# A feed-forward stage with half of its features turned by DMA transposes as two float16 numbers

## The chip, the cores and the metric

The kernel runs on one core of a Trainium2 chip. The metric is the device time of one execution in microseconds (us), the median of several runs. A NeuronCore has five engines that run their own queues of instructions in order: PE (TensorE, matrix products; the load of its stationary operand is shown apart as PEld), DVE (VectorE), ACT (ScalarE), POOL (GpSimd) and SP (SyncE, which here only issues DMA transfers). They meet through semaphores: an instruction waits until others have signalled.

## The reference

The reference is a small graph network of two layers over 4096 nodes with 256 features. Each layer is an attention over a 4096 x 4096 adjacency followed by a feed-forward. The change touches only the feed-forward of layer 0, which applies one step 30 times to every row:

```python
def step(h, _):
    h = h + 0.01 * jnp.tanh(h)
    h = h * jax.nn.sigmoid(h)
    h = _layernorm(h, ln_w, ln_b)        # (h - mean) * rsqrt(var + EPS) * w + bias
    h = jnp.einsum('bsc,dc->bsd', h, W) + b
    return (h, None)
x, _ = jax.lax.scan(step, x, None, length=N_ITERS)      # 30 steps
# the layer: x = x + that of layernorm(x)
```

All inputs and the result are float32.

## The kernel before

The kernel is written with a recording layer: each line appends an instruction to an engine's queue, tiles come from pools with a number of buffers (`bufs`), and waits for data and for free buffers are put in automatically. Before the change a scheduler of that layer may move instructions of one engine past each other where it thinks that it helps.

The feed-forward keeps all 4096 rows in SBUF, in the tile `y` (128 partitions, 32 row tiles `NT`, 256 columns; scaled by 100, so that the factor 0.01 can be folded into the activations). The rows are cut into `NG` = 8 groups of `G` = 4 row tiles, 512 rows. One group in one step is a **unit**; there are 30 x 8 = 240, numbered so that all groups do step 1, then all do step 2. The loop over `at` is a software pipeline, in which several units are at different places at once. A unit goes through:

- L772, ACT: the tanh of `y` into `th`, 1024 columns a partition; L773, POOL: `th + y`.
- L778, ACT: the silu of that into `z`.
- L101 and L103, DVE (in the helper `over_std`): `bn_stats` and `bn_aggr` of each row; L105, DVE: EPS added to the variances, 4 columns; L106, POOL: the power -0.5 of them, which gives `ln_rstd`.
- L114, PE (in the helper `transposed`): eight transposes of 128x128 blocks of `z` into the PSUM tile `tp`; L813, ACT: its copy into `zT`. The matmul contracts over features, so these must lie on the partitions.
- L787, PE: eight float32 matmuls with 256 columns, two blocks of the contraction (`KC` = 2) for each of four row tiles, into `po`. In the trace each is two matmul instructions.
- L797, DVE: `po` times `ln_rstd` plus `bias`, back into `y`, four operations of 256 columns.

The weights `wT` are prepared ahead of the loop (L731 to L754): the norm's weights and bias are folded into them, and the mean over the features is taken off, so that the norm's subtraction isn't needed. `init` (L712 to L716) norms the rows of a group as they come in from DRAM, during the first eight turns of the loop. In the last step, `last` stands for `bias`, and L807 adds the layer's input rows (DVE) before they are stored to DRAM; the attention of layer 1 begins with them.

In the attention, lines L394 (DVE, two inputs in SBUF), L337 and L368 (POOL), L328, L335 and L483 (ACT), and L569 (PE, float16 matmuls with 130 columns) serve below as measured examples of operations of like kind.

Of the kernel before, what the change touches and what calls it, by code (L numbers as in the profile page):

```python
# [11 lines left out]
F32 = mybir.dt.float32  # L12
BF16 = mybir.dt.bfloat16
F16 = mybir.dt.float16
I32 = mybir.dt.int32
AF = mybir.ActivationFunctionType
OP = mybir.AluOpType
AX = mybir.AxisListType
# [3 lines left out]
P = 128  # L22
C = 256
KC = C // P
# [3 lines left out]
G = 4  # L28
EPS = 1e-5
# [6 lines left out]
TINY = 1e-30  # L36


def bcast_rows(ap, n=P):

    return bass.AP(tensor=ap.tensor, offset=ap.offset, ap=[[0, n]] + [list(x) for x in ap.ap])
# [3 lines left out]
def gnn_ffn_kernel(ctx: ExitStack, tc: tile.TileContext, a: dict, out: bass.AP):  # L45
    nc = tc.nc
# [3 lines left out]
    NG = NT // G  # L50
    GR = G * P
# [44 lines left out]
    def over_std(pool, src):  # L96

        st = pool.tile([P, G, 6], F32, name="ln_st")
        mv = pool.tile([P, G, 2], F32, name="ln_mv")
        for r in range(G):  # L100
            nc.vector.bn_stats(st[:, r, :], src[:, r, :])  # L101
        for r in range(G):
            nc.vector.bn_aggr(mv[:, r, :], st[:, r, :])  # L103
        rstd = pool.tile([P, G], F32, name="ln_rstd")
        nc.vector.tensor_scalar(rstd, mv[:, :, 1], EPS, None, op0=OP.add)  # L105
        nc.gpsimd.tensor_tensor(rstd, rstd, mhalf, OP.pow)  # L106
        return rstd, mv

    def transposed(psum, src, name="tp"):

        ps = psum.tile([P, KC, GR], F32, name=name)
        for k in range(KC):
            for r in range(G):
                nc.tensor.transpose(ps[:, k, r * P : (r + 1) * P], src[:, r, k * P : (k + 1) * P], ident)  # L114
        return ps
# [573 lines left out]

    with ExitStack() as scope:
        one = scope.enter_context(tc.tile_pool(name="f_one", bufs=1))
        wT = one.tile([P, KC, C], F32, name="wT")
        bias = one.tile([P, C], F32, name="bias")
        last = one.tile([P, C], F32, name="last")
        y = one.tile([P, NT, C], F32, name="y")
        work = scope.enter_context(tc.tile_pool(name="f_work", bufs=3))
        small = scope.enter_context(tc.tile_pool(name="f_small", bufs=6))

        x1 = {}

        def load(g):
            if g not in ahead:
                load_ahead(x1d, g)
            x1[g] = ahead.pop(g)

        def init(g):
            t = x1.pop(g)
            rstd, mv = over_std(small, t)  # L710
            rs = small.tile([P, G], F32, name="rs")
            nc.vector.tensor_scalar(rs, rstd, 100.0, None, op0=OP.mult)  # L712
            nm = small.tile([P, G], F32, name="nm")
            nc.vector.scalar_tensor_tensor(nm, mv[:, :, 0], -1.0, rs, op0=OP.mult, op1=OP.mult)
            for r in range(G):
                nc.scalar.activation(  # L716
                    y[:, g * G + r, :], t[:, r, :], AF.Identity, scale=rs[:, r : r + 1], bias=nm[:, r : r + 1]
                )

        load(0)  # L720
        load(1)
        with tc.tile_pool(name="f_prep", bufs=1) as prep, tc.tile_pool(name="f_pps", bufs=1, space=PSUM) as pps:
            ln = prep.tile([2 * KC, P], F32, name="ln")
            nc.scalar.dma_start(ln[:KC], a["L0_ffn_ln_w"].rearrange("(k p) -> k p", p=P))
            nc.scalar.dma_start(ln[KC:], a["L0_ffn_ln_b"].rearrange("(k p) -> k p", p=P))
            wr = prep.tile([P, KC, C], F32, name="wr")
            nc.scalar.dma_start(wr, a["L0_ffn_W"].rearrange("(k p) c -> p k c", p=P))
            nc.scalar.dma_start(bias, bcast_rows(a["L0_ffn_b"]))
            init(0)
            ps = pps.tile([P, 2 * KC], F32, name="ps_ln")  # L730
            nc.tensor.transpose(ps, ln, ident[: 2 * KC, : 2 * KC])  # L731
            lnT = prep.tile([P, 2 * KC], F32, name="lnT")
            nc.vector.tensor_scalar(lnT, ps, 100.0, None, op0=OP.mult)
            lbb = prep.tile([P, KC, P], F32, name="lbb")
            nc.vector.tensor_copy(lbb, lnT[:, KC:, None].to_broadcast([P, KC, P]))
            ps = pps.tile([P, KC, C], F32, name="ps_w")
            for k in range(KC):
                for o in range(KC):
                    nc.tensor.transpose(ps[:, k, o * P : (o + 1) * P], wr[:, o, k * P : (k + 1) * P], ident)
            raw = prep.tile([P, KC, C], F32, name="raw")  # L740
            nc.vector.tensor_copy(raw, ps)
            ps = pps.tile([P, C], F32, name="ps_b")
            for k in range(KC):
                nc.tensor.matmul(ps, lbb[:, k, :], raw[:, k, :], start=(k == 0), stop=(k == KC - 1))
            nc.vector.scalar_tensor_tensor(bias, bias, 100.0, ps, op0=OP.mult, op1=OP.add)

            nc.vector.tensor_scalar(last, bias, -100.0, None, op0=OP.add)
            for k in range(KC):
                nc.vector.tensor_scalar(raw[:, k, :], raw[:, k, :], lnT[:, k : k + 1], None, op0=OP.mult)
            ps = pps.tile([P, C], F32, name="ps_m")  # L750
            for k in range(KC):
                nc.tensor.matmul(ps, mean, raw[:, k, :], start=(k == 0), stop=(k == KC - 1))
            for k in range(KC):
                nc.vector.tensor_tensor(wT[:, k, :], raw[:, k, :], ps, OP.subtract)  # L754

        ps_t = scope.enter_context(tc.tile_pool(name="f_pst", bufs=2, space=PSUM))
        ps_o = scope.enter_context(tc.tile_pool(name="f_pso", bufs=2, space=PSUM))

        th, zs, rs, zT = {}, {}, {}, {}
        units = FFN_STEPS * NG  # L760
        for at in range(units + 4):
            if at < NG:
                if at + 2 < NG:
                    load(at + 2)
                if at:
                    init(at)
            if units - NG <= at - 1 < units:
                load((at - 1) % NG)
            if at < units:
                g = at % NG  # L770
                th[at] = work.tile([P, G, C], F32, name="th")
                nc.scalar.activation(th[at], y[:, g * G : (g + 1) * G, :], AF.Tanh, scale=0.01)  # L772
                nc.gpsimd.tensor_tensor(th[at], th[at], y[:, g * G : (g + 1) * G, :], OP.add)  # L773
            if 0 <= at - 2 < units:
                pt = transposed(ps_t, zs.pop(at - 2))
            if 0 <= at - 1 < units:
                z = zs[at - 1] = work.tile([P, G, C], F32, name="z", bufs=4)
                nc.scalar.activation(z, th.pop(at - 1), AF.Silu, scale=0.01)  # L778
                rs[at - 1] = over_std(small, z)[0]
            if 0 <= at - 3 < units:  # L780
                u = at - 3
                g = u % NG
                src = zT.pop(u)
                po = ps_o.tile([P, G, C], F32, name="po")
                for r in range(G):
                    for k in range(KC):
                        nc.tensor.matmul(  # L787
                            po[:, r, :],
                            src[:, k, r * P : (r + 1) * P],
                            wT[:, k, :],  # L790
                            start=(k == 0),
                            stop=(k == KC - 1),
                        )
                rstd = rs.pop(u)
                end = u >= units - NG
                for r in range(G):
                    nc.vector.scalar_tensor_tensor(  # L797
                        y[:, g * G + r, :],
                        po[:, r, :],
                        rstd[:, r : r + 1],  # L800
                        last if end else bias,
                        op0=OP.mult,
                        op1=OP.add,
                    )
                if end:
                    t = x1.pop(g)
                    nc.vector.scalar_tensor_tensor(  # L807
                        t, y[:, g * G : (g + 1) * G, :], 0.01, t, op0=OP.mult, op1=OP.add
                    )
                    nc.sync.dma_start(rows_of(x2d, g), t)  # L810
            if 0 <= at - 2 < units:
                zT[at - 2] = work.tile([P, KC, GR], F32, name="zT")
                nc.scalar.copy(zT[at - 2], pt)  # L813


    RH = a["L1_ffn_router_w1"].shape[1]
# [456 lines left out]
```

## Time and profile before

| | |
|---|---|
| median of 3 runs | 3517.87 us (3514.87 to 3520.3) |
| profiled execution | span 3522.9 us, mean clock of TensorE 0.977 of full |
| the feed-forward's matmuls (L787) | first at 812.36, last ends at 1877.63 us |
| of one unit, mean durations | L772 1047 ns, L773 2367, L778 1060, L101 414 (x4), L103 154 (x4), L105 302 (median), L106 1019 (median), L813 1011, L797 470 (x4) |
| other rows used below | L807 1210 ns (1024 columns), L394 1233 (1040 columns), L368 240, L328 582 (512 columns from PSUM), L335 301, L483 712 (512 columns) |

Over the whole span the page gives PE 92% busy, DVE 85%, ACT 75%, POOL 32%. These are averages over stages with different limits, so the feed-forward has to be read by itself.

In a line of a timeline the columns are: start in us, how long in us, engine, line, operation, what it writes and reads with shapes, how many in a row, and in brackets how long the engine sat idle before it and who ended that wait. Operations of one engine overlap a little at their ends (about 0.08 us on DVE), so durations of instructions in a row add up to somewhat more than the time that they take. In the chain of waits, a line is a start, a length, and the engine and line that the end of the stretch hung on.

### The profile page before, as it was taken

How to read it: one execution, taken by the hardware profiler on the slowest of the kernel's cores; microseconds unless marked ns; L12 is line 12 of the kernel's file. 1: busy time of each engine (PE TensorE's matmuls, PEld its weight loads, DVE VectorE, ACT ScalarE, POOL GpSimd, SP SyncE). 2: the span in 40 equal slices, each digit the busy share in tenths (PEclk: the TensorE clock that was granted, in tenths of full speed). 3: DMA queues.
4: the chain of work that ended last, by engine and by line, in shares of the span. 5: the costliest groups of instructions: out<-in, count | busy, mean ns of one | idle time of the engine just before them, and what ended most of it. 6: DMA issues, size and time to landing. Idle time of an engine off the chain costs nothing.

```text
span 3522.9 us, 80529 instructions
## 1 busy us (share of the span) xinstructions
PE 3251.1 (92%) x33403; PEld 2927.4 (83%) x33403; DVE 3009.0 (85%) x6007; ACT 2638.3 (75%) x2934; POOL 1136.6 (32%) x899
## 2 busy tenths in 40 slices
PE   7889999996999999999999899999989999995995
PEld 4788888885888888888886799999879999984784
DVE  7999999997877777777778899999889999996445
ACT  3888888886766666666664999999799999982221
POOL 4111001005877777777772000000120000002662
PEclk9999999998999999999999999999999999997997
DMA  7997786501000000000006030321313140414224
GB/s 148 174 221 172 161 205 127 161 23 55 1 1 1 1 1 1 1 1 1 1 1 228 17 115 29 115 85 59 117 61 102 57 133 26 127 50 144 82 89 182
DMA packets 280198, 288.44 MB, mean 82 GB/s; under 512 B 97149, under 2 KB 230426, under 8 KB 279834
## 3 DMA queue, kind: packets, MB, share of 16 engines
q1 hardware_dynamic: 198770, 224.18, 19.3%
q0 software_dynamic: 73920, 52.97, 9.9%
q10 hardware_dynamic: 7144, 6.16, 0.6%
q8 instruction: 263, 4.31, 0.5%
q14 instruction: 101, 0.83, 0.1%
HBM read 248.01 MB, written 68.81 MB: 90 GB/s over the span
## 4 chain that ended last, share of the span: by engine, by line
PE 40%; DVE 33%; issue 14%; POOL 5%; ACT 5%; DMA 2%; another core or an unknown queue 0%; ACTq 0%; DVEq 0%; POOLq 0%; SPq 0%
PE po L787 22%; DVE m L617 17%; PE acc L569 9%; PE tp L114 6%; ACT st L483 3%; DVE rows L632 3%; DVE m L632 2%; POOL yd L1193 2%; POOL gx L1127 2%; DVE v L382 1%; DVE u L496 1%; DVE ms L229 1%; DVE u L506 1%; DVE u L510 1%; DVE u L518 1%
## 5 line engine op out<-in xcount | busy, mean ns | idle before, releaser
L569 PE MATMUL acc<-vals,m 128*128 128x130 f16 (+1 forms) x19456 | 1721.2, 232 | 73.0 <-DVE m L632 43.4
L483 ACT ACTIVATE st<-f1b,f2b 128x1024 bf16<-128x1024 f32 (+2 forms) x1664 | 1659.1, 1073 | 98.2 <-DVE m L617 91.7
L569 PEld LDWEIGHTS <-m 128*128 128x128 bf16 x19456 | 1516.2, 98 | 171.1 <-DVE m L632 65.9
L617 DVE TENSOR_TENSOR m<-st,m 128x2048 bf16<-128x2048 bf16 (+2 forms) x832 | 928.9, 1134 | 15.0 <-ACT st L483 14.9
L787 PE MATMUL po<-wT,zT 128*128 128x256 f32 x3840 | 874.5, 381 | 13.5 <-ACT zT L813 12.5
L787 PEld LDWEIGHTS po<-wT,zT 128*128 128x128 f32 x3840 | 713.7, 191 | 104.6 <-ACT zT L813 15.0
L773 POOL TENSOR_TENSOR th<-th,y 128x1024 f32<-128x1024 f32 x240 | 567.9, 2367 | 192.7 <-ACT th L772 192.7
L569 PE MATMUL acc<-vals,rows 128*128 128x130 f16 x5120 | 614.3, 221 | 15.3 <-DVE rows L632 15.3
L106 POOL TENSOR_TENSOR ln_rstd<-ln_rstd,mhalf 128x4 f32<-128x4 f32 x272 | 286.8, 1055 | 872.1 <-DVE ln_rstd L105 652.6
L569 PEld LDWEIGHTS <-rows 128*128 128x128 bf16 x5120 | 490.1, 96 | 20.8 <-DVE rows L632 20.4
L101 DVE BATCH_NORM_STATS2 ln_st<-z 128x6 f32<-128x256 f32 x960 | 337.9, 414 | 190.6 <-ACT z L778 190.6
L813 ACT COPY zT<-tp 128x1024 f32<-128x1024 f32 x240 | 242.8, 1011 | 323.1 <-PE tp L114 323.1
L632 DVE TENSOR_TENSOR rows<-m,m 128x2048 bf16<-128x2048 bf16 x320 | 391.7, 1224 | 10.2
L797 DVE SCALAR_TENSOR_TENSOR y<-po,ln_rstd,bias 128x256 f32<-128x256 f32 x928 | 378.7, 470 | 5.7 <-PE po L787 4.9
L778 ACT ACTIVATE z<-th 128x1024 f32<-128x1024 f32 x240 | 254.3, 1060 | 18.1 <-POOL th L773 17.8
L114 PE MATMUL tp<-ident,z 128*128 128x128 f32 x1920 | 250.1, 273 | 9.0 <-ACT z L778 8.1
L772 ACT ACTIVATE th<-y 128x1024 f32<-128x1024 f32 x240 | 251.2, 1047 | 4.8 <-DVE y L797 4.8
L114 PEld LDWEIGHTS tp<-ident,z 128*128 128x128 f32 x1920 | 224.9, 141 | 35.9 <-ACT z L778 10.7
L209 POOL DMA_DIRECT2D rows<-in_adj_dram x80 | 72.9, 912 | 490.9 <-PE tp_m L219 478.3
L632 DVE TENSOR_TENSOR m<-m,m 128x1792 bf16<-128x1792 bf16 (+1 forms) x200 | 202.2, 1011 | 13.0 <-PE acc L569 0.5
L462 POOL MEMSET hs<- 128x4 f32 x3 | 0.3, 102 | 603.4 <-DVE u L513 583.1
L1155 ACT COPY w<-ew 128x512 f32 x37 | 22.7, 618 | 129.1 <-PE ph L1162 66.5
(217 smaller groups left out, 2420.1 us busy)
## 6 DMA issues: line engine op xcount, KB each, us to landing
m<-edges SPq DMA_DIRECT2D x32, 2048.0 KB
rows<-in_adj_dram POOLq DMA_DIRECT2D x64, 448.0 KB
edges<-ms SPq DMA_DIRECT2D x64, 448.0 KB
m<-edges SPq DMA_DIRECT2D x16, 1792.0 KB
f1b<-fd SPq DMA_DIRECT2D x32, 512.0 KB
rows<-x1d SPq DMA_DIRECT2D x16, 512.0 KB
y<-yd SPq DMA_DIRECT2D x16, 512.0 KB
f1b<-fd SPq DMA_DIRECT2D x16, 448.0 KB
```

Of the source, the lines that this page charges most:

```text
L101: nc.vector.bn_stats(st[:, r, :], src[:, r, :])
L106: nc.gpsimd.tensor_tensor(rstd, rstd, mhalf, OP.pow)
L114: nc.tensor.transpose(ps[:, k, r * P : (r + 1) * P], src[:, r, k * P : (k + 1) * P], ident)
L483: nc.scalar.activation(steps[at][:, s, :w], f1b[c, h][:, :w], AF.Relu, bias=f2b[:, 2 * q + s, h : h + 1], scale=BIG)
L569: nc.tensor.matmul(acc[:, i, cols], lhs[:, s, rows], v[:, cols], start=(j == 0 and n_ == 0), stop=(j == NT - 1 and n_ == 1), skip_group_ch ...
L617: nc.vector.tensor_tensor(m1[:, :, :w], st[:, :, :w], m, OP.logical_and if turned(q) else OP.min)
L632: nc.vector.tensor_tensor(m2[:, :, :w], m, m1[:, :, :w], OP.subtract)
L772: nc.scalar.activation(th[at], y[:, g * G : (g + 1) * G, :], AF.Tanh, scale=0.01)
L773: nc.gpsimd.tensor_tensor(th[at], th[at], y[:, g * G : (g + 1) * G, :], OP.add)
L778: nc.scalar.activation(z, th.pop(at - 1), AF.Silu, scale=0.01)
L787: nc.tensor.matmul(po[:, r, :], src[:, k, r * P : (r + 1) * P], wT[:, k, :], start=(k == 0), stop=(k == KC - 1),)
L797: nc.vector.scalar_tensor_tensor(y[:, g * G + r, :], po[:, r, :], rstd[:, r : r + 1], last if end else bias, op0=OP.mult, op1=OP.add,)
```

## The change

The contraction of 256 features is cut in two halves. The first 128 features are turned by PE as before: four transposes for a unit, one float32 matmul for each row tile. The second 128 features leave PE's transposes. Each value of `z` there is scaled by a power of two and written as the sum of two float16 numbers: ACT makes the upper one (rounded), DVE the remainder, the lower one, in one operation that reads `z` and the upper half. One DMA transpose, issued by SP, turns both, 128 x 1024 float16 numbers, from SBUF to SBUF. The weights of this half are also split in two float16 numbers, and four float16 matmuls (upper and lower of `z` with upper and lower of the weights) take the place of one float32 matmul. The purpose is to take transposes off PE.

The rest goes with it:

- The scales are found from the weights and the bias ahead of the loop, so that float16 can't overflow; `under`, their inverse, is multiplied into the row factors by POOL.
- EPS is added by ACT, no longer by DVE.
- POOL's addition of `th` gets a wait for the lower half's operation on DVE.
- The loop's instructions on PE, DVE, ACT and POOL stand in written order; no scheduler moves them.
- The pipeline is one turn deeper: transposes at `at - 3`, matmuls at `at - 4`, `y` at `at - 5`.
- In the last step the factor 0.01 is in `last` and `under`, and POOL adds the layer's input, no longer DVE.
- Three groups of rows, not two, are asked for ahead, and their norms are measured a turn earlier.

```diff
-        wT = one.tile([P, KC, C], F32, name="wT")
+        wT = one.tile([P, C], F32, name="wT")
+        w16 = one.tile([P, 2, C], F16, name="w16")
...
-            nc.vector.tensor_scalar(last, bias, -100.0, None, op0=OP.add)
+            nc.vector.tensor_scalar(last, bias, -100.0, 0.01, op0=OP.add, op1=OP.mult)
...
+            nc.vector.tensor_tensor(sq, raw, raw, OP.mult)
...
+                nc.tensor.matmul(ps, mean, sq[:, k, :], start=(k == 0), stop=(k == KC - 1))
...
+            nc.vector.tensor_reduce(far[:, 0:1], ps, axis=AX.X, op=OP.max)
...
+            nc.gpsimd.tensor_tensor(far[:, 1:2], far[:, 0:1], mhalf[:, :1], OP.pow)
...
+            nc.vector.tensor_scalar(wT, raw[:, 0, :], scale[:, :1], scale[:, 1:], op0=OP.mult, op1=OP.mult)
+            nc.vector.tensor_scalar(w16[:, 0, :], raw[:, 1, :], scale[:, 1:], None, op0=OP.mult)
+            nc.vector.scalar_tensor_tensor(
+                w16[:, 1, :], raw[:, 1, :], scale[:, 1:], w16[:, 0, :], op0=OP.mult, op1=OP.subtract
+            )
...
-        for at in range(units + 4):
+        with tc.manual_schedule(engines={PE, DVE, Activation, Pool}):
+            for at in range(units + 6):
...
+                u = at - 3
+                    for r in range(G):
+                        nc.tensor.transpose(pt[:, r * P : (r + 1) * P], z[:, r, :P], ident)
+                u = at - 5
+                    for r in range(G):
+                        nc.vector.scalar_tensor_tensor(y[...], po[:, r, :], rstd[:, r : r + 1], last if end else bias, ...)
+                u = at - 2
+                    nc.scalar.activation(z, th.pop(u), AF.Silu, scale=0.01)
+                    z16 = work.tile([P, 2, G, P], F16, name="z16", bufs=4)
+                    nc.scalar.activation(z16[:, 0], z[:, :, P:], AF.Identity, scale=scale[:, :1])
+                    lower = nc.vector.scalar_tensor_tensor(
+                        z16[:, 1], z[:, :, P:], scale[:, :1], z16[:, 0], op0=OP.mult, op1=OP.subtract
+                    )
+                    zT16[u] = work.tile([P, 2 * G, P], F16, name="zT16", bufs=4)
+                    nc.sync.dma_start_transpose(zT16[u], z16.rearrange("p s r c -> p (s r c)"))
+                if at < units:
+                    nc.scalar.activation(th[at], y[:, g * G : (g + 1) * G, :], AF.Tanh, scale=0.01)
+                    ins = nc.gpsimd.tensor_tensor(th[at], th[at], y[:, g * G : (g + 1) * G, :], OP.add)
+                    if lower is not None:
+                        tc.add_manual_dep(ins.ins, lower.ins.name, ..., reason="the port that both use")
...
+                u = at - 3
+                    nc.scalar.copy(zT[u], pt)
+                    nc.scalar.activation(rs[u], mvs.pop(u)[:, :, 1], AF.Identity, bias=eps)
+                    nc.gpsimd.tensor_tensor(rs[u], rs[u], mhalf, OP.pow)
+                    nc.gpsimd.tensor_tensor(rs[u], rs[u], under[:, int(u >= units - NG), :], OP.mult)
...
+                u = at - 4
+                    for r in range(G):
+                        nc.tensor.matmul(po[:, r, :], src[:, r * P : (r + 1) * P], wT, start=True, stop=False)
+                        for part in range(2):
+                            for other in range(2):
+                                nc.tensor.matmul(po[:, r, :], src16[:, part * G + r, :], w16[:, other, :], ...)
...
-                    nc.vector.scalar_tensor_tensor(
-                        t, y[:, g * G : (g + 1) * G, :], 0.01, t, op0=OP.mult, op1=OP.add
-                    )
+                    nc.gpsimd.tensor_tensor(t, t, y[:, g * G : (g + 1) * G, :], OP.add)
```

## The prediction

> **What bounds the kernel now.** I went from the page to the stage. The page's table by 40 slices shows one stage, from about 800 to 1880 us, with PE at 9 tenths in nearly every slice and no DMA traffic; it is the feed-forward. So I read the table by stretches in the middle of it (PE, PEld, DVE, ACT, POOL busy, granted clock, DMA share, GB/s), then the chain of waits of the same stretch in order of time.
>
> ```profile
> 1200.00:1400.00 200.00, 200.00 (x1110) 178.64 (x1109) 159.46 (x601) 134.94 (x140) 156.61 (x93) 1.00 0.00 1
> ```
> ```profile
> 1203.16 0.87 PE tp L114 x8
> 1204.04 3.46 PE po L787 x16
> 1207.49 0.87 PE tp L114 x8
> 1208.36 3.46 PE po L787 x16
> ```
>
> PE is busy for all of the 200 us at full clock, and the chain holds nothing but PE: a unit (512 rows, one step) is 8 transposes in 0.87 us and 16 matmul instructions in 3.46 us, together a **period of 4.33 us**, 240 times 1039 us. Per instruction that is 109 ns a transpose and 216 ns a float32 matmul instruction of 256 columns (two for each matmul of the source). The others per period, from the first line times 4.33/200: DVE 3.45, POOL 3.39, ACT 2.92 us. PE is the bound, but DVE and POOL are only a fifth below it, and the change loads both.
>
> The timeline of one period, and one from the attention after this stage, show a second coupling:
>
> ```profile
> 1302.37 2.37 POOL L773 TENSOR_TENSOR th<-th,y 128x1024 f32<-128x1024 f32 x1 [0.84 <-ACT th L772]
> ...
> 1304.46 0.30 DVE L105 TENSOR_SCALAR ln_rstd<-ln_mv 128x4 f32<-128x4 f32 x1
> ...
> 1304.84 1.02 POOL L106 TENSOR_TENSOR ln_rstd<-ln_rstd,mhalf 128x4 f32<-128x4 f32 x1
> ```
> ```profile
> 1902.46 1.23 DVE L394 SCALAR_TENSOR_TENSOR vals<-vals,v 128x1040 f16<-128x1040 f16 x1
> 1902.72 1.84 POOL L106 TENSOR_TENSOR ln_rstd<-ln_rstd,mhalf 128x4 f32<-128x4 f32 x1 [3.23 <-DVE ln_rstd L105]
> ...
> 1903.69 1.23 DVE L394 SCALAR_TENSOR_TENSOR vals<-vals,v 128x1040 f16<-128x1040 f16 x1
> ```
>
> In the first, the tiny EPS addition on DVE ends at 1304.76, just as POOL's long addition ends at 1304.74; it takes 0.30 us where it elsewhere takes 0.15. In the second, the power on POOL takes 1.84 instead of 1.02 us: it waits until DVE's two-input operation ends at 1903.69. But the next two-input operation then runs its usual 1.23 us beside the rest of that power. So the power holds what they share only for a moment, not for its whole 1.02 us.
>
> **What the Trainium skill says.** "SBUF — State Buffer", section "Who interferes with whom", says that a DVE instruction with two SBUF inputs and a GpSimd instruction that reads SBUF exclude each other, and the second waits. The trace agrees with the wait (0.82 us above), but the power lets go early. "DMA: Bandwidth & Descriptors", section "Latency and other measured facts", gives 261 GB/s for DMA transposes in one kernel; "VectorE: DVE Perf Modes", section "The three transpose paths", gives 1309 ns for one 128x128 transpose by DMA. No run here has a DMA transpose. "TensorE: Matmul & The Clock Gate", section "Wait — 56ns, not 53.3ns?", gives N columns / 2.4 GHz + 2.5 ns for a bf16 matmul. The 216 ns of a float32 instruction of 256 columns fits two such passes.
>
> **The change, part by part, for one unit.**
>
> PE loses 4 of 8 transposes: 0.435 us remains. Half of the contraction stays float32: 8 instructions, 3.46/2 = 1.73 us. The other half becomes 16 float16 matmuls of 256 columns. Low bound by the TensorE page: 109 ns. High bound by the nearest row, the attention's float16 matmul of 130 columns: 109 of them in 7.81 us at 784.82 us, 72 ns each, scaled by columns 141 ns. I take 109, since 72 ns for 130 columns must hold a fixed part (the weight load), which 256 columns hide: 16 x 0.109 = 1.75 us. **PE: 0.435 + 1.73 + 1.75 = 3.91 us** (4.43 at the high bound).
>
> DVE loses the EPS addition (0.30, of which 0.21 alone) and gains the lower half's two-input operation, 512 columns: from the rows of 256 columns (470 ns) and 1024 columns (1210 ns, L807) 0.96 ns a column, 0.72 us, or 0.64 back to back. 3.45 - 0.21 + 0.64 = **3.88 us**, within 1% of PE.
>
> ACT gains the upper half (512 columns with a pointer scale: 0.58 to 0.71 us by the copies of 512 columns and the 712 ns of L483) and the EPS addition (0.30 by L335), and its copy of the turned half shrinks from 1.01 to 0.58: 2.92 - 0.43 + 0.6 to 0.7 + 0.2 to 0.3 is about 3.4 us. Hidden under PE.
>
> POOL keeps 2.37 + 1.02 and gains a multiply of 4 columns, 0.24 us by L368: 3.63 us plus gaps, about **3.75 us**. Its long addition now waits for the lower half. Behind it on POOL queue the power and the multiply, for which the y of two steps later waits. Once DVE has done the lower half, it needs bn_stats, bn_aggr and y (1.32 + 0.28 + 1.54 = 3.14 us) before it wants the next one, and the addition is over after 2.37 + 0.1. So they interleave; only the multiply may be held up some 0.2 us, and POOL still closes its round in under 3.9.
>
> The DMA transpose (256 KB in, 256 KB out) is new, on an idle queue. Its latency L, from the lower half's end to data in place, is the great unknown. The queue before holds nothing it would wait for. In written order a ring closes over three steps: lower half of unit u, transpose, matmuls of u, y of u, lower half of u+3 behind it on DVE. Hence 3T >= L + 3.46 + 1.63 + 0.72 + about 0.4 of hand-overs, **T >= (L + 6.2)/3**. With T = 3.91 it stays hidden up to L = 5.5 us; T is back at 4.33 with L = 6.8. Low bound: 1.0 us of data at 261 GB/s plus 1.3, L = 2.3. High bound: eight 128x128 blocks one after another, 8 x 1.309 = 10.5 us. I take about 4 us, since blocks spread over 16 DMA engines should overlap; both ends stay in the range.
>
> Written order itself costs nothing in the steady state as long as each engine has slack in its step. I take T = 3.95 rather than 3.91 for hand-overs between four engines that all stand at 3.4 to 3.9: 240 x (4.33 - 3.95) = **91 us gained**.
>
> Outside the steady state: before, the first matmul stands at 812.36 and the last ends at 1877.63, 1065 us for 1039 us of periods, so 26 us go in the start, waiting for loads and the initial norms. The preparation gets a serial chain: square, a matmul at low clock (1.2), a maximum, a power (1.0), some dozen tiny DVE operations (0.15 each plus hand-overs), the splitting of the weights: about 8 us ahead of the first upper half. One step more of pipeline and L delay the first matmul by about 4 us more. Part lies beside the loads; I book 8 us. The last sums go from DVE (1.21 us each) to POOL (2.37 by L773); only the last is exposed, and the next stage waits for its store: 2 us. Sum: 3517.9 - 91 + 8 + 2 = **3437 us**.
>
> **Rivals.**
>
> Small gain. Four engines near the same load with in-order waits do not mesh, T = 4.2: -31 + 10, about 3497. For it: DVE at 3.88 has no slack, and each wait for another engine breaks its back-to-back overlap of 0.08 us. Against it: before, 190 us of DVE idle time had one cause, ACT's z, and it recovered every period.
>
> The transpose bounds, slower. L = 8 gives T = 4.73: +97 + 10, about 3625; L = 10.5, or a queue that takes one transpose only after another, T = 5.6 and some 3830. For it: nothing in the trace shows the rate, and the 261 GB/s are of another kernel. Against it: the DMA engines are idle in this stage.
>
> PE or the shared port bounds, slower. Float16 at 141 ns gives T = 4.43; power and multiply keeping DVE's lower half out for their whole length gives 2.37 + 1.02 + 0.24 + 0.72 + 0.1 = 4.45. Either: +29 + 10, about 3556. Against: the 1.23 us at 1903.69, and the fixed part in 72 ns.
>
> **How the numbers follow.** Forecast 0.61, small gain 0.13, transpose 0.18, PE or port 0.08. Faster by over 0.2% (under 3511) takes the first and most of the second: 0.72. Within 0.2%: 0.03, where small gain and a transpose near L = 6.8 meet. Slower: 0.25. The forecast's spread is 3400 (T = 3.91 and a start no longer than before) to 3465 (T = 4.05). Upward the range must take in the third rival, to 3570; beyond lies most of the transpose case, 0.17.
>
> **What would show it.** Right: in mid-stage PE still 100% busy, pieces of 4 transposes in 0.44 us and 20 matmuls' worth in 3.47 us, DVE above 95%, POOL's addition released by the lower half, and no matmul released by a DMA. Wrong: idle time ahead of the matmuls with the turned float16 tile as releaser (transpose); float16 matmuls of over 120 ns (PE); the lower half on DVE longer than 0.8 us or the power longer than 1.1 us in every period (port); a first matmul later than 830 us (preparation).

## The result and the profile after

The changed kernel takes **3432.9 us** (median of 4 runs, 3431.05 to 3437.91), the kernel before 3519.1 us in the same comparison. The ratio is **0.9759, 95% interval 0.9742 to 0.9776**: 86 us faster.

The table by stretches, middle of the stage (PE, PEld, DVE, ACT, POOL busy, granted clock, DMA share, GB/s), of the changed kernel:

```profile
1200.00:1400.00 200.00, 200.00 (x1430) 163.75 (x1429) 199.68 (x665) 173.44 (x256) 191.42 (x154) 1.00 0.38 68
```

PE is still never idle, and now DVE is busy for 99.8% and POOL for 95.7% of the time. The chain of waits of the changed kernel, one unit from it:

```profile
1201.61 0.44 PE tp L831 x4
1202.05 0.43 PE po L896 x2
1202.48 0.44 PE po L899 x4
1202.92 0.43 PE po L896 x2
1203.35 0.44 PE po L899 x4
...
1205.53 0.44 PE tp L831 x4
```

Four transposes, then four times two float32 instructions and four float16 ones: 1201.61 to 1205.53 is a period of **3.92 us** where it was 4.33. Sixteen float16 matmuls take 4 x 0.44 us, 109 ns each; the loads of their stationary operands (98 ns each in the trace) run beside them and add nothing. The timeline of the same kernel shows how the other engines fit in:

```profile
1301.30 0.74 DVE L853 SCALAR_TENSOR_TENSOR z<-z,scale,z 128x512 f16<-128x512 f32 x1
1301.69 0.41 POOL L886 TENSOR_TENSOR z_rs<-z_rs,under 128x4 f32<-128x4 f32 x1
...
1302.18 2.37 POOL L862 TENSOR_TENSOR th<-th,y 128x1024 f32<-128x1024 f32 x1
...
1304.50 1.01 POOL L885 TENSOR_TENSOR z_rs<-z_rs,mhalf 128x4 f32<-128x4 f32 x1
...
1305.22 0.74 DVE L853 SCALAR_TENSOR_TENSOR z<-z,scale,z 128x512 f16<-128x512 f32 x1
```

The lower half (L853) runs undisturbed, 0.74 us. The multiply (L886) comes while it runs and takes 0.41 us instead of the 0.20 that it takes in e7 and e12. It ends at 1302.10, and the long addition follows at 1302.18, with the way free: the next lower half starts 0.67 us after the addition's end, while the power runs, and is not held up by it. Below, "what the two share" stands for whatever it is that makes a two-input operation of DVE and an operation of POOL wait for each other.

No matmul waits for a DMA from 1200 to 1400 us. In a table by quarters of a microsecond the transposes show only as bursts of about 1.4 us on the DMA engines; the burst of the lower half that ended at 1302.04 is over at about 1304.7.

### The profile page after: what moved, and what is told of

It reads as the page before. It is cut to its first block, busy times and chain, and to the rows that moved or that the text cites. A ratio compares the mean times of both kernels' runs of the same rounds, so it can differ in the third digit from the quotient of the medians.

```text
span 3430.3 us, 84143 instructions
## 1 busy us (share of the span) xinstructions
PE 3156.7 (92%) x34367; PEld 2771.3 (81%) x34367; DVE 3115.3 (91%) x6016; ACT 2754.3 (80%) x3414; POOL 1242.3 (36%) x1149
## 4 chain that ended last, share of the span: by engine, by line
PE 36%; DVE 35%; issue 13%; POOL 7%; ACT 6%; DMA 2%; DVEq 0%; POOLq 0%; ACTq 0%; SPq 0%
DVE m L617 17%; PE acc L569 10%; PE po L899 9%; PE po L896 9%; ACT st L483 4%; DVE rows L632 3%; PE tp L831 2%; DVE m L632 2%; POOL th L862 2%; PE ph L1262 1%; POOL yd L1293 1%; DVE z_st L874 1%; DVE y L838 1%; POOL gx L1227 1%; DVE u L496 1%
## 5 line engine op out<-in xcount | busy, mean ns | idle before, releaser
L899 PE MATMUL po<-w,zT 128*128 128x256 f16 x3840 | 580.4, 274 | 5.7 <-DMA zT<-z 5.7
L896 PE MATMUL po<-wT,zT 128*128 128x256 f32 x1920 | 579.1, 384 | 6.4 <-ACT zT L881 6.4
L899 PEld LDWEIGHTS <-zT 128*128 128x128 f16 x3840 | 377.6, 98 | 169.7 <-DMA zT<-z 7.3
L838 DVE SCALAR_TENSOR_TENSOR y<-po,z_rs,bias 128x256 f32<-128x256 f32 x928 | 384.8, 477 | 4.2 <-PE po L899 2.1
L874 DVE BATCH_NORM_STATS2 z_st<-z 128x6 f32<-128x256 f32 x960 | 335.5, 412 | 0.0
L896 PEld LDWEIGHTS po<-wT,zT 128*128 128x128 f32 x1920 | 292.5, 193 | 16.4 <-ACT zT L881 7.8
L106 POOL TENSOR_TENSOR ln_rstd<-ln_rstd,mhalf 128x4 f32<-128x4 f32 x32 | 42.1, 1317 | 656.8 <-DVE ln_rstd L105 641.9
L850 ACT ACTIVATE z<-th 128x1024 f32<-128x1024 f32 x240 | 251.2, 1046 | 7.3 <-POOL th L862 6.6
L885 POOL TENSOR_TENSOR z_rs<-z_rs,mhalf 128x4 f32<-128x4 f32 x240 | 244.5, 1019 | 0.0
L881 ACT COPY zT<-tp 128x512 f32<-128x512 f32 x240 | 140.8, 587 | 116.2 <-PE tp L831 116.2
```

What stands on the lines that cost most here:

```text
L838: nc.vector.scalar_tensor_tensor(y[:, g * G + r, :], po[:, r, :], rstd[:, r : r + 1], last if end else bias, op0=OP.mult, op1=OP.add,)
L850: nc.scalar.activation(z, th.pop(u), AF.Silu, scale=0.01)
L874: nc.vector.bn_stats(st[:, r, :], z[:, r, :])
L885: nc.gpsimd.tensor_tensor(rs[u], rs[u], mhalf, OP.pow)
L896: nc.tensor.matmul(po[:, r, :], src[:, r * P : (r + 1) * P], wT, start=True, stop=False)
L899: nc.tensor.matmul(po[:, r, :], src16[:, part * G + r, :], w16[:, other, :], start=False, stop=(part == 1 and other == 1),)
```

## The experiments

The ratios below are to the kernel before, in the same comparison, since from one comparison to the next its median moved by up to 15 us (3508 to 3523). A time "against the changed kernel" is the difference of the two ratios times 3520 us; with the intervals as they are, a difference of less than some 7 us can't be told from none.

### Where the gain comes from: PE, and the order

**e1_all_on_pe.** All transposes and float32 products back on PE, the rest of the change kept (without a lower half, POOL's addition has nothing to wait for on DVE).

```diff
-                    for r in range(G):
-                        nc.tensor.transpose(pt[:, r * P : (r + 1) * P], z[:, r, :P], ident)
+                    pt = transposed(ps_t, z)            # eight transposes
...
-                    (z16, lower, dma_start_transpose; four float16 matmuls per row tile)
+                    (two float32 matmuls per row tile, L787's form)
```

> All 256 features turned by PE again, all products float32; no float16 halves, no DMA transposes. Kept: written order, EPS on ACT, the multiply and the last sums on POOL, the longer preparation. Theory (the gain is PE's lighter load): the period goes back to 4.33 us, 240 x (4.33 - 3.92) = 98 us above the changed kernel, about 3531 us, so some 12 us slower than before, since the longer start and end stay. Rival (written order or the EPS move brought the gain): stays below 3480 us.

Measured: 3524.3 us (3521.2 to 3530.7), ratio 1.0006 (0.9997 to 1.0015): no difference from before. The middle of the stage:

```profile
1200.00:1400.00 200.00, 200.00 (x1113) 178.72 (x1112) 150.34 (x555) 142.63 (x185) 165.67 (x139) 1.00 0.00 1
```

PE is never idle and does 1110 to 1113 matmul instructions in 200 us, as before the change. So written order, EPS on ACT and the sums on POOL bring nothing by themselves; the steady gain is the four transposes that PE no longer does. The 12 us that I expected for a longer start and end are not there: 2 us, interval -1 to 5.

**e2_scheduler.** The changed kernel without the written order.

```diff
-        with tc.manual_schedule(engines={PE, DVE, Activation, Pool}):
+        if True:
```

> The changed kernel without the written order: the scheduler may move instructions of PE, DVE, ACT and POOL. Theory (with PE at 100, DVE at 99.8 and POOL at 96 per cent there is no slack for an order that puts another operation ahead): 20 to 80 us slower than the changed kernel, 3453 to 3513 us. Rival (order hardly matters, the loads decide): within 6 us of 3433.

Measured: 3657.8 us (3655.9 to 3660.3), ratio 1.0385 (1.0368 to 1.0402): 4% slower than the kernel before, and 220 us slower than the changed kernel, nearly three times what I allowed at most. Its timeline shows why:

```profile
1299.44 2.35 POOL L855 TENSOR_TENSOR th<-th,y 128x1024 f32<-128x1024 f32 x1
1299.57 2.77 DVE L846 SCALAR_TENSOR_TENSOR z<-z,scale,z 128x512 f16<-128x512 f32 x1
...
1304.57 0.67 PE L889 MATMUL po<-wT,zT 128*128 128x256 f32 x2 [1.61 <-DVE z_mv L869]
```

The scheduler moves every second lower half so far back that another unit's addition on POOL starts just before it: it then takes 2.77 us, all behind it on DVE is late, and PE waits. From 1200 to 1400 us the 41 lower halves take 1.78 us on average where they took 0.74, 1.04 us more; the period over the 200 middle units is 4.85 us where it was 3.92, 0.93 more. So this wait accounts for the loss, and the chain of waits of this stretch holds hardly any PE. With the order that this scheduler chose the transposes lose; they gain with an order that keeps these two operations apart.

**e3_eps_on_dve.** EPS back on DVE, behind `bn_aggr`.

```diff
-                    nc.scalar.activation(rs[u], mvs.pop(u)[:, :, 1], AF.Identity, bias=eps)
+                    nc.vector.tensor_scalar(rs[u], mvs.pop(u)[:, :, 1], EPS, None, op0=OP.add)
```

> EPS added by DVE again, in the written place behind bn_aggr, nothing else changed. Theory (the small fp32 operation is shut out by POOL's long addition, which runs from the end of the lower half for 2.37 us): a period is the sum of lower half 0.66, hand-over 0.14, addition 2.37, EPS 0.15, y 1.54, hence 4.86 us, +225 us, about 3658 us, and L884's operation takes about 1 us on DVE. Rival (only DVE's load counts): 0.15 us more a period, +36 us, about 3470 us.

Measured: 3633.0 us, ratio 1.0314 (1.0293 to 1.0334), +195 us. Groups by line (busy, mean ns) in the stretch from 1200 to 1400 us:

```profile
L884 DVE TENSOR_SCALAR z_rs<-z_mv 128x4 f32<-128x4 f32 x43 | 43.9, 1021 | 0.0
```

Four columns take 1.02 us on average instead of 0.15; each ends when POOL's addition ends. The period is 4.75 us, by the sum on record 4.86. In the kernel before, the same operation cost 0.30 us and nothing on the bound, since there it met only the last 0.28 us of the addition. What makes this tiny operation dear is the moment at which it comes, and the new order moves that moment. The move to ACT is therefore no detail of the change: without it, in this order, the change loses.

**e4_no_port_wait.** The explicit wait taken out.

```diff
-                    if lower is not None:
-                        tc.add_manual_dep(ins.ins, lower.ins.name, ...)
```

> The wait of POOL's addition for the lower half is taken out (the two share no data). Theory (the two exclude each other and POOL's addition is ready 2.4 us earlier, at the end of the tanh): the addition starts first, the lower half is held up by it, and the period becomes 4.2 to 4.35 us, +65 to +105 us, 3500 to 3540 us, with the lower half at 1.2 us or more instead of 0.74. Rival (POOL and DVE fall into step by themselves): within 10 us of 3433.

Measured: 3439.6 and 3461.0 us, ratio 0.9795 (0.9759 to 0.9831). The steady period stays at 3.92 us, with 200.00 of 200 us on PE. The profile is of the run of 3439.6 us, and its stage is over as early as that of the changed kernel; why the other run took 21 us more is open, and with two runs so far apart a small cost of leaving the wait out can't be excluded. My theory of a longer period was wrong, and the timeline shows what I left out:

```profile
1302.47 0.74 DVE L853 SCALAR_TENSOR_TENSOR z<-z,scale,z 128x512 f16<-128x512 f32 x1
1302.72 0.55 POOL L879 TENSOR_TENSOR z_rs<-z_rs,under 128x4 f32<-128x4 f32 x1
...
1303.23 2.37 POOL L862 TENSOR_TENSOR th<-th,y 128x1024 f32<-128x1024 f32 x1
```

The multiply stands ahead of the addition in POOL's queue and is itself held until the lower half ends (0.55 us). So in this order the addition doesn't come too early: the small operation does the work of the wait. The explicit wait is a safeguard, not the source of the gain.

### What bounds now

**e5_less_pe** leaves out the product of the two lower halves, **e6_less_dve** half of the statistics, **e7_less_both** both.

```diff
-                        for part in range(2):
-                            for other in range(2):
+                        for part, other in ((0, 0), (0, 1), (1, 0)):        # e5, e7
...
-                    for r in range(G):
+                    for r in range(0, G, 2):                                # e6, e7
                         nc.vector.bn_stats(st[:, r, :], z[:, r, :])
```

> Left out: the product of the two lower halves, so three float16 matmuls instead of four for each row tile; PE has 0.44 us less a period, 3.48 us. Theory (DVE at 99.8 per cent is a second bound right below PE): the period falls only to DVE's 3.90 us, at most 6 us less than the changed kernel, 3427 to 3433 us. Rival (PE alone bounds, DVE's business is partly waiting): down to POOL's 3.76 us or lower, 38 us or more less, below 3395 us.

> Left out: the statistics of every second row tile (its neighbour's are used), so DVE has two bn_stats less a period, 0.7 us. Theory (PE bounds): the period stays at 3.92 us, within 5 us of the changed kernel, 3428 to 3438 us, with DVE at about 82 per cent. Rival (DVE bounds and PE's queue only looks full): faster by 20 us or more.

> Both of these left out. Theory (two bounds next to each other, POOL is the third): the period falls to POOL's round, 2.37 + 1.02 + 0.20 and its gaps, 3.65 to 3.8 us, 30 to 65 us less than the changed kernel, 3370 to 3403 us. Rival (each of the two alone bounds nothing, the ring over the DMA transpose does): stays within 10 us of 3433.

e5: 3413.5 us (3410.1 to 3415.6), ratio 0.9701 (0.9685 to 0.9717), 20 us less than the changed kernel, between the two expectations (at most 6, and 38 or more). The middle of the stage:

```profile
1200.00:1400.00 200.00, 194.94 (x1264) 149.12 (x1262) 200.00 (x687) 178.72 (x264) 191.10 (x158) 1.00 0.41 71
```

The period is 3.80 us, and the chain of waits is DVE almost throughout. So DVE is the next bound, 3% below PE, where I had put it at 0.5%. Where the 0.12 us were hidden, two timelines show, first of the changed kernel, then of e5:

```profile
1303.27 0.36 DVE L876 BATCH_NORM_AGGREGATE z_mv<-z_st 128x2 f32<-128x6 f32 x4
1303.64 1.66 DVE L838 SCALAR_TENSOR_TENSOR y<-po,z_rs,bias 128x256 f32<-128x256 f32 x4
```
```profile
1302.90 0.37 DVE L876 BATCH_NORM_AGGREGATE z_mv<-z_st 128x2 f32<-128x6 f32 x4
1303.18 1.63 DVE L838 SCALAR_TENSOR_TENSOR y<-po,z_rs,bias 128x256 f32<-128x256 f32 x4
```

In e5 `y` starts 0.09 us before the last `bn_aggr` ends: operations of one engine overlap at their ends. In the changed kernel `y` starts only after that end, so this overlap is lost: `y` starts 0.37 us behind the first `bn_aggr` instead of 0.28, which is 0.09 of the 0.12 us. DVE is waiting there, though the table counts it as busy. (With less for DVE to do, in e6 below, this wait comes into the open: DVE waits 32 us of the 200 at `y` for PE's products.)

e6: 3430.6 us (3425.5 to 3431.4), ratio 0.9747 (0.9731 to 0.9763), within the noise of the changed kernel, as the theory said, with DVE busy for 83% and the period at 3.92 us. PE bounds the changed kernel.

e7: 3459.8 us (3453.6 to 3461.3), ratio 0.9836 (0.9820 to 0.9852): **slower** than each of the two, with less work than either. Neither theory had that. Its timeline:

```profile
1302.57 2.37 POOL L862 TENSOR_TENSOR th<-th,y 128x1024 f32<-128x1024 f32 x1
...
1304.23 1.26 DVE L853 SCALAR_TENSOR_TENSOR z<-z,scale,z 128x512 f16<-128x512 f32 x1
...
1304.90 1.47 POOL L885 TENSOR_TENSOR z_rs<-z_rs,mhalf 128x4 f32<-128x4 f32 x1
...
1306.44 0.20 POOL L886 TENSOR_TENSOR z_rs<-z_rs,under 128x4 f32<-128x4 f32 x1
...
1306.59 2.36 POOL L862 TENSOR_TENSOR th<-th,y 128x1024 f32<-128x1024 f32 x1
```

DVE, with less to do and not held back by PE, is at its lower half before the addition ends (1304.94). It waits (1.26 us), gets what the two share ahead of the power, and now the power waits (1.47 instead of 1.02 us). Addition, lower half, rest of the power, multiply follow each other: 4.02 us.

**e12_stats_first** tests that reading: e7's work, but on DVE the statistics ahead of the lower half.

```diff
                     nc.scalar.activation(z16[:, 0], ...)
+                    (bn_stats, bn_aggr)
                     lower = nc.vector.scalar_tensor_tensor(z16[:, 1], ...)
...
-                    (bn_stats, bn_aggr)
```

> As e7_less_both (the product of the lower halves and half of the statistics left out), but DVE takes the statistics ahead of the lower half. In e7 DVE is so early that its lower half waits for the end of POOL's addition (1.26 instead of 0.74 us) and then goes ahead of the power, which waits in its turn (1.46 instead of 1.02): addition, lower half, rest of the power and multiply one after another, 4.02 us. Theory (it is this order at what both share): with 0.7 + 0.3 us of statistics first, the lower half comes just behind the start of the power, which holds up nothing any more, and the period falls to POOL's own round, 3.65 to 3.75 us, 65 to 90 us less than e7: a ratio of 0.958 to 0.966 to the kernel before, 3370 to 3400 us where before takes 3519. Rival (something else holds e7 at 4.02): within 12 us of e7, a ratio of 0.980 to 0.987.

Measured: 3360.6 us (3358.8 to 3362.0), ratio **0.9539 (0.9523 to 0.9555)**, 105 us less than e7 by the ratios, with the same instructions. That is even below the range on record (0.958 to 0.966). Its timeline:

```profile
1301.26 2.37 POOL L869 TENSOR_TENSOR th<-th,y 128x1024 f32<-128x1024 f32 x1
...
1303.59 1.01 POOL L884 TENSOR_TENSOR z_rs<-z_rs,mhalf 128x4 f32<-128x4 f32 x1
1303.86 0.72 DVE L860 SCALAR_TENSOR_TENSOR z<-z,scale,z 128x512 f16<-128x512 f32 x1
1304.68 0.20 POOL L885 TENSOR_TENSOR z_rs<-z_rs,under 128x4 f32<-128x4 f32 x1
1304.84 2.36 POOL L869 TENSOR_TENSOR th<-th,y 128x1024 f32<-128x1024 f32 x1
```

The lower half starts 0.27 us after the power and lies wholly beside it; neither is longer than alone. POOL works almost without a gap, 3.58 us a period, and is the bound. The 0.45 us that the power waited in e7 (1.47 against 1.02) are the whole difference of the two periods, 4.02 and 3.58. It is the order at what the two share, and not the amount of work, that made e7 slow. (e6, e7 and e12 leave out needed statistics and are no versions to use.)

### The slack of the DMA transpose

**e8_late_lower.** The lower half one turn later.

```diff
                 u = at - 2      # silu, upper half
...
+                u = at - 3
                     lower = nc.vector.scalar_tensor_tensor(zl16[:, 1], zl[:, :, P:], ...)
                     nc.sync.dma_start_transpose(zT16[u], ...)
```

> The lower half of a unit is made one turn later (same work), so that the DMA transpose has one turn instead of two before the matmuls. With the DMA traffic of the changed kernel (bursts of about 1.4 us that end some 2.8 us after the lower half's end) I put L at 2.8 us. Theory (the ring of waits, now over two turns: L, matmuls behind the first float16 one 3.03, y 1.66, lower half 0.66, hand-overs 0.3): period (2.8 + 5.65) / 2 = 4.2 us, +70 us, 3480 to 3520 us, with PE's float16 matmuls waiting for the DMA in each period. Rival (L is so short that one turn is enough): within 8 us of 3433. If L were the 4 us of the prediction: period 4.8 us, 3640 us.

Measured: 3579.2 us, ratio 1.0174 (1.0153 to 1.0194), slower than expected (3480 to 3520 us). From 1200 to 1400 us matmuls wait 24 us for the transpose, and the loads of their stationary operands 36 us. The period is 4.55 us on average (44 units in 200 us). From the timeline L can be read where a matmul waits:

```profile
1299.37 10.04 SPq L861 DMA_TRANSPOSE zT<-z  x3
...
1302.46 0.61 PE L904 MATMUL po<-w,zT 128*128 128x256 f16 x4 [0.77 <-DMA zT<-z]
```

The first transpose is released at 1299.37, just as the lower half ends, and its matmul starts at 1302.46: **L = 3.1 us**. The ring gives (3.1 + 5.65) / 2 = 4.4 us, and the turns come in pairs of 3.9 and 4.9 us whose mean is just that. What makes 4.55 of it is that L isn't always 3.1, as three pieces of the chain of waits show:

```profile
1202.38 4.45 DMA zT<-z
1212.58 3.04 DMA zT<-z
1221.38 3.75 DMA zT<-z
```

Of the 24 waits of a float16 matmul for a transpose in this stretch, 15 end 3.1 to 3.2 us after the lower half's end and 9 end 3.5 to 4.9 us after it, and the turns with these take 5.2 to 5.6 us. Among the DMA packets of this trace from 930 to 1700 us, all 20 bursts of the transpose that last over 1.8 us overlap packets of the queues that load instructions, and 22 of the 150 shorter ones do. That points to a cause; no run here tests it.

With two turns, as the change has it, the slack is 3.9 us more, and even the longest L seen, 4.9 us, is under the 5.5 us of the prediction's ring. That is why nothing waits there.

### Start and end

**e9_sums_split** puts the last sums of the first three groups on DVE, **e10_factors_early** writes the row factors of `init` at the head of a turn, **e11_best** has both, and e5's omission.

```diff
-                    nc.gpsimd.tensor_tensor(t, t, y[...], OP.add)
+                    (nc.vector if at < units else nc.gpsimd).tensor_tensor(t, t, y[...], OP.add)   # e9, e11
...
             for at in range(units + 6):
+                if at + 1 < NG:
+                    factors(at + 1)                # rs and nm, taken out of init; e10, e11
```

> The last sums of the first three groups go to DVE, the other five stay on POOL. In the changed kernel these three turns take 6.3 us instead of 3.92, since POOL then has two long additions (2 x 2.37 + 1.02 + 0.20). Theory (POOL bounds these turns): with the sums on DVE they take DVE's 3.9 + 1.2 us and some waiting behind POOL's addition, 3 to 5 us less, 3428 to 3430 us. Rival (the sum on DVE is shut out by POOL's addition and holds up all behind it): no gain, 3432 to 3437 us.

> In the first turns the row factors of the incoming group (L726 and L728, tiny DVE operations) are written at the head of the turn, ahead of the lower half, so ahead of POOL's addition. In the changed kernel they are shut out by that addition (2.31 and 2.24 us in the preparation, 0.7 to 1.1 us in the turns) and ACT waits 16 us in all for them before it can bring rows in. Theory (this chain sets the 7.4 us turns of the start): 6 to 14 us less, 3419 to 3427 us. Rival (the start waits for the rows' loads or ACT's own work): within 4 us of 3433.

> Both of these, and the product of the two lower halves left out as in e5_less_pe (three float16 matmuls for each row tile). Theory (steady state, start and end are separate stretches and their savings add): 19 + 6 to 14 + 3 to 5 us less than the changed kernel, 3395 to 3405 us. Rival (what is won at the start or end was waiting for the same thing): 3405 to 3414 us.

e9: 3423.2 us (3420.7 to 3425.4), ratio 0.9758 (0.9745 to 0.9772): no gain that stands out of the noise, and the wait that the rival expected is there. The sum has two inputs in SBUF and meets POOL's addition, in its timeline:

```profile
1760.76 2.36 POOL L862 TENSOR_TENSOR th<-th,y 128x1024 f32<-128x1024 f32 x1
...
1762.13 2.08 DVE L912 TENSOR_TENSOR rows<-rows,y 128x1024 f32<-128x1024 f32 x1
1763.08 1.99 POOL L885 TENSOR_TENSOR z_rs<-z_rs,mhalf 128x4 f32<-128x4 f32 x1
```

2.08 instead of 1.2 us, the power behind it 1.99: turns of 5.8 us instead of 6.3. By the last products of the attention's preparation (L308, at 1850.29 against 1852.09) 2 us of that are left.

e10: 3414.1 us (3411.0 to 3415.4) in the same comparison as e9, which equals the changed kernel: 9 us less, ratio 0.9731 (0.9718 to 0.9745). In the changed kernel the start has lines like these (timeline; the first two are in the preparation, the others in a turn of the loop):

```profile
803.31 2.31 DVE L726 TENSOR_SCALAR rs<-ln_rstd 128x4 f32<-128x4 f32 x1 [0.33 <-POOL ln_rstd L106]
...
809.21 2.24 DVE L728 SCALAR_TENSOR_TENSOR nm<-ln_mv,rs 128x4 f32<-128x4 f32 x1
...
829.00 1.10 DVE L726 TENSOR_SCALAR rs<-ln_rstd 128x4 f32<-128x4 f32 x1
...
830.33 2.07 ACT L730 ACTIVATE y<-rows,nm,rs 128x256 f32<-128x256 f32 x4 [2.01 <-DVE nm L728]
```

Operations of four columns take 1.1 to over 2.2 us, since they wait for POOL's addition, and ACT waits for them. e10 leaves the two in the preparation as they are (2.30 and 2.24 us); in the turns the factors now stand ahead of the addition and take 0.17 us each. ACT waits 8 instead of 16 us for them, and the first matmuls of the 21st unit start at 916.24 instead of 923.57.

e11: 3390.2 us (3387.3 to 3392.2), ratio **0.9667 (0.9654 to 0.9681)**: the fastest version that keeps the computation but for the product of the two lower halves, 32 us ahead of the changed kernel, which was expected to be 28 to 38. The savings add: 20 of e5, 10 of e10 and none to speak of from e9.

## Why the prediction was right

3437 was forecast, 3432.9 came. The mechanism is the one that was forecast: PE still bounds, and its period falls by the four transposes. That the sum came within 4 us is partly luck, as the points on start and end show. Point by point:

- **PE's 3.91 us a unit**: 3.92 measured. The choice of 109 ns for a float16 matmul of 256 columns, against 141, was right: 16 in 1.75 us. The formula that the Trainium skill gives for bf16 ("TensorE: Matmul & The Clock Gate", section "Wait — 56ns, not 53.3ns?") comes to 109 ns for 256 columns, and the trace agrees for float16.
- **DVE 3.88**: too high by 0.08; it is 3.80 when it bounds (e5). The lower half took 0.74 us, 0.72 was forecast. So DVE had a margin of 3% to PE, not 1%, and the hand-overs, for which I added 0.03 us a period, cost nothing: 7 us of the sum.
- **ACT 3.4 and POOL 3.75**: 200 us hold 51 units with 173.44 us of ACT's work and 191.42 us of POOL's, so 3.40 and 3.75 us, as forecast; the multiply is held up by 0.2 us, as forecast. One sign on record isn't seen: the trace shows POOL's addition behind the multiply, and not released by the lower half. The lower half holds up the multiply (e4).
- **L of about 4 us**: 3.1 us in most and up to 4.9 us in some of the turns of e8, under the 5.5 that the steady state allows. The rival with eight blocks one after another, 10.5 us, is refuted.
- **What the two share**: that a power, once begun, holds up nothing, taken from two lines of the attention, decided for the forecast, and e12 shows it in the stage itself. But a power that comes while DVE's operation runs waits for it. The rival of 4.45 us, with all of it one after another, was not wrong in kind: e7 has its chain at 4.02 us. In the changed kernel PE's period keeps the lower half late enough: it does so even where DVE has less to do (e6), and no longer where PE has less to do as well (e7).
- **Written order**: "costs nothing in the steady state" was too weak. It is what makes the change a gain (e2, against the order that the scheduler chose).
- **Start and end, 10 us**: too small by about 6. The last products of the attention's preparation (L308) start at 1852.09 instead of 1933.64: 82 us are left of the 98 that 240 periods gain.
- **Of these 16 us, the start** cost 5 at most, where 8 were booked. The first matmul stands at 828.17 instead of 812.36, but that is no loss of 16 us, since the kernel before has its waits behind its first matmul (turns of up to 9.3 us, against 7.4). At the 21st unit the changed kernel is 3 us ahead (923.57 against 926.80), where 20 periods gain 8. e1, with the same preparation and its first matmul at 827.49, is as early there (923.49) with the old period. The row factors, which I had not looked at, are held up in the kernel before too (2.30 us at 813.87), so what e10 wins on them is a chance that was left rather than a cost of the change. (Also, `y` comes two turns later than before, at `at - 5` instead of `at - 3`; "one turn deeper" holds for the transposes and the matmuls.)
- **The end** cost some 12 us, where 2 were booked. At the 221st unit the changed kernel is 85 us ahead (1707.56 against 1792.64). The 20 periods that follow should add 8; instead it loses 1 by its last matmul (1793.3 against 1877.63) and 3 more on the way to L308. Some 7 of the 12 lie in three turns of the end (6.1 to 6.3 instead of 3.92 us), where POOL has two long additions in one turn. I wrote that only the last sum is exposed. The last unit's matmuls also wait 1.8 us for their transpose.
- **What cancels**: start and end took about 6 us more than booked, the hand-overs 7 us less. That is the luck in the 4 us.
- The medians differ by 86 us, and the two profiled executions by 92.6 us (3522.9 and 3430.3), since that of the kernel before took 7 us more than its median. Of the 92.6, some 8 arise after 3200 us, in the last stage, whose gathers the change doesn't touch. I leave these few microseconds open.

## What to carry to other kernels

When several engines stand within a few per cent of the bound, ask of each pair that can shut each other out which comes first in a period: the same instructions gave 0.984 or 0.954 of the time before, 105 us apart, by their order alone (e7, e12), and taking work away made a kernel slower. Look for tiny operations on an engine whose neighbour runs long instructions: where the two exclude each other, as here, the price of the tiny one is the neighbour's remaining time, and it changes when any change moves the moment at which it comes. The DMA transpose beside the bound engine cost nothing in the steady state, since its latency fits in the turns of the pipeline; measure that latency by taking a turn away, and look at the slowest of them and not only at the usual one.

## What was unexpected of the hardware

- A DMA transpose of 128 x 1024 float16 numbers, SBUF to SBUF, took 3.1 us from release to use in most turns and up to 4.9 us in some (e8), 1.23 us of SP's queue for its issue, and a burst of about 1.4 us on the DMA engines. What runs beside it is not longer than in the kernel before: `bn_stats` 412 ns against 414, the silu 1046 against 1060, a transpose on PE 109 ns in both.
- The power of four columns on POOL takes 1.02 us. It waits for a two-input operation of DVE that came first (e7: 1.47 us), but once begun it doesn't hold one up (e12: 0.72 us of it, within the power's 1.01 us). The long addition holds it up until its end (e2: 2.77 us instead of 0.74).
- DVE at 99.8% busy still had 3% to give (3.92 to 3.80 us in e5): a wait of less than the overlap of two operations leaves no idle time in the table. Being busy is not being the bound.
